# A fused cross-attention, Mamba and expert layer on one core: late matmul groups in the weighted values' PSUM bank, the joining of context blocks cut in four, three scalings in one step, first queries' transposes issued earlier

## The chip, the cores and the metric

One core of a Trainium2 chip. The kernel is one launch with no collectives. The metric is the device time of one execution in microseconds, as a median of repeated runs; beside it stands one profiled execution, from which all durations of single instructions are taken.

## The reference, cut to what matters

All data are fp32. Sixteen sequences of 128 rows and width 512 each attend to a context of 2048 rows; then each pair of sequences goes through a Mamba layer (a scan over time with 16 states for each of 1024 channels), an MLP, and a mixture of experts.

```python
x = x + xattn(layernorm(x), ctx)        # 16 heads of 32; q,k,v,o projections of 512x512
x = x + mamba_block(layernorm(x))       # in_proj, causal conv of 4, SiLU, dt/B/C, scan, out_proj,
                                        # rmsnorm, MLP 512-2048-512 with exact GELU, rmsnorm
x = x + experts(layernorm(x))           # shared matmul + expert matmul times a gate's weight
# attention, for sequence b:
q = layernorm(x[b]) @ wq.T + bq;  k = ctx[b] @ wk.T + bk;  v = ctx[b] @ wv.T + bv
out = softmax(q k^T / sqrt(32)) v  @ wo.T + bo
```

## The kernel before, in words

**Units.** The program is one long unrolled list. Its loop `for u in range(last)` writes one *unit* after the other; the first 256 (NU) are the attention's. Unit u works on sequence b = u // 16, on the context block of 512 rows sb = u // 4 % 4, and on the group of four heads hg = u % 4. A *row* below is the 16 units of one sequence; row 12 is units 192 to 207. Every engine takes its instructions strictly in the order in which they were written, under `tc.manual_schedule()`, so this loop is the schedule.

**What a unit issues, in order.** `scores` (L302): four matmuls q k^T into the four PSUM banks `banks[0..3]`. `weighted` of the unit before (L346): the probabilities times v, summed over a whole sequence's head group into the bank `avp`; after the fourth head group `avp` is copied to SBUF (`avs`, L360), which happens in units with u % 4 == 0. The `head` list. `maxima` (L310, VectorE): the negated row maximum of each of the four banks. `x_products` (L240): two products for the next context block's keys or values, into the banks `pa` and `pc` (a Strassen-Winograd scheme: seven products of quarter size for each of k and v, spread over units; its sums of context quarters t1 to t4 are GpSimd's, L232, in units with u % 4 == 1). `exps` (L320, ScalarE). Then the Mamba part of an earlier pair of sequences, which runs 22 units behind: `inputs` (L639, GpSimd), `decays` (L660, ScalarE), `scan` (L674 and L677, VectorE; L690, GpSimd). `x_sums` (VectorE, reads `pc`). `turn` (L333): the probabilities are transposed, four transposes for each of i = 0 to 3, each i into one of the four banks, and copied out as `pT` (L338, ScalarE; i = 2 on VectorE, L336, in units with u % 16 > 2). The lists `middle`, `late`, `behind`, `after`, `inner`. Last `y_products` (one or two more products) and `y_sums`, and `silu_second` (L565, VectorE).

**The lists.** `put(list, u, f)` hangs a piece of work on a unit. A `late` piece is a group of matmuls with its own PSUM result: in an attention unit it gets `banks[3]`, a second one `banks[0]`, and so on; only turns 0 to 2 go before it, and turn 3 is issued after it, into the bank behind the last one used. The late pieces are `turned` (L389, the normalised x transposed, copied out by VectorE as xnT, L391), `queries` (L399), `scaled` (L455, a factor for each head transposed, which VectorE multiplies onto `avs`, L460 and L462, and GpSimd adds up into aT, L463), `attended` (the output projection, L468), `z_turned` (L515), `x_part` and `z_part` (L522), `x_proj` (L576), `projected` (L703). `behind` (dt_first, L606) uses `pc`.

**The end of a sequence.** With e = 16 b + 16 the four blocks' maxima and sums are joined: `joined` gathers the maxima with four copies (L422), takes their minimum (L427) and the differences (L428); `shares` is an exponential; `joined_second` (L436 to L438) sums; `joined_third` (L443) divides. `spread_out` (L449, GpSimd) widens the factors into the tile `fx`, which has two buffers and also holds xnT.

**The start of a sequence.** With s = 16 b: load x at s - 8, `moments_of` (L66) at s - 7, `root_of` and `normal` (L83, L89 to L91, L376, and GpSimd's x + bo, L380) at s - 6, `turned` at s - 5, `queries` at s - 4. Sequence 0 has these in the stretch before the loop, where `turned(0, banks[3])` comes after the sums of the weights' quarters (`weight_sums`, L216 to L219) of k and of v.

**After the loop's attention part** the program goes on with the MLP, the experts and the last scans; there PSUM banks come from a free list.

Of the kernel before, what the change touches and what calls it, by code (L numbers as in the profile page):

```python
# [34 lines left out]
def perceiver_layer(ctx: ExitStack, tc: tile.TileContext, a: dict, out: bass.AP):  # L35
# [73 lines left out]
    with ExitStack() as es:  # L109
# [254 lines left out]
        def moments_of(b):  # L364
            moments(keep, mv[:, b, :], xts[b])
            xts[b, "r"] = root_first(keep, mv[:, b, 1:2], 1e-5)

        def root_of(b):
            root_second(*xts[b, "r"])

        def normal(b):

            x = xts[b]
            root_third(rstd[:, b : b + 1], *xts.pop((b, "r")))
            xn = keep.tile([P, D], FP, tag="aT", name="xn", bufs=1)
            nc.vector.tensor_scalar(  # L376
                xn, x, mv[:, b, 0:1], rstd[:, b : b + 1], ALU.subtract, ALU.mult
            )
            if b:
                nc.gpsimd.tensor_tensor(x, x, bo, ALU.add)  # L380
            xts[b, "n"] = xn
            nm = [keep.tile([P, SB, 4], FP, tag=f"nm{j}", name=f"nm{b}_{j}") for j in range(4)]
            sm = keep.tile([P, SB, H], FP, tag="sm", name=f"sm{b}")
            stats[b] = nm, sm

        def turned(b, ps):
            xn = xts.pop((b, "n"))
            for kc in range(KC):
                nc.tensor.transpose(heads(ps)[:, kc, :], xn[:, kc * P : (kc + 1) * P], ident)  # L389
            xnT = keep.tile([P, KC, P], FP, tag="fx", name="xnT")  # L390
            nc.vector.tensor_copy(xnT, heads(ps))  # L391
            xts[b, "t"] = xnT

# [23 lines left out]
        def joined(b):  # L417

            parts, sm = stats[b]
            nm = keep.tile([P, SB, H], FP, tag="nm", name=f"nm{b}")  # L420
            for j in range(4):
                nc.vector.tensor_copy(  # L422
                    nm.rearrange("p s (k j) -> p s k j", j=4)[:, :, :, j], parts[j]
                )
            lo = keep.tile([P, 1, H], FP, tag="lo", name="lo")
            flat = lo.rearrange("p a h -> p (a h)")
            nc.vector.tensor_reduce(flat, nm.rearrange("p s h -> p h s"), AX.X, ALU.min)  # L427
            nc.vector.tensor_tensor(nm, lo.to_broadcast([P, SB, H]), nm, ALU.subtract)  # L428
            stats[b] = nm, sm, lo, flat

        def shares(b):
            nc.scalar.activation(stats[b][0], stats[b][0], AF.Exp)
# [12 lines left out]
        fxs = {}  # L445

        def spread_out(b, sb):
            fx = keep.tile([P, H, HD], FP, tag="fx", name="fx")
            nc.gpsimd.tensor_copy(fx, stats[b][:, sb, :].unsqueeze(2).to_broadcast([P, H, HD]))  # L449
            fxs[b, sb] = fx.rearrange("p h d -> p (h d)")  # L450

# [199 lines left out]
        def anew(h):  # L651

            nc.vector.memset(h.rearrange("p n (b t) -> p (n b) t", b=GB)[:, :, 0:1], 0.0)  # L653
# [423 lines left out]
        def put(where, u, f):  # L1077
            where.setdefault(u, []).append(f)

        for b in range(B):  # L1080
            s = 16 * b
            if b:
                put(loads, s - 8, lambda b=b: load_x(b))
                put(loads, s - 5, lambda b=b: load_w(0, b))
                put(inner, s - 7, lambda b=b: moments_of(b))
                put(middle, s - 6, lambda b=b: root_of(b))
                put(inner, s - 6, lambda b=b: normal(b))
                put(late, s - 5, lambda ps, b=b: turned(b, ps))
                put(late, s - 4, lambda ps, b=b: queries(b, ps))
            e = s + 16  # L1090
            put(loads, e + 5, lambda b=b: load_w(3, b))
            put(inner, e - 1, lambda b=b: joined(b))
            put(middle, e, lambda b=b: shares(b))
            put(head, e + 1, lambda b=b: joined_second(b))
            put(head, e + 2, lambda b=b: joined_third(b))
            for sb in range(SB):
                put(inner, e + 2 + sb // 2, lambda b=b, sb=sb: spread_out(b, sb))
                put(late, e + 3 + sb // 2, lambda ps, b=b, sb=sb: scaled(b, sb, ps))
            put(late, e + 6, lambda ps, b=b: attended(b, ps))
            put(middle, e + 7, lambda b=b: root_of(b))  # L1100
            put(inner, e + 7, lambda b=b: normed(b))
            put(late, e + 8, lambda ps, b=b: z_turned(b, ps))
        for g in range(NG):
# [15 lines left out]
            for i in range(GB):  # L1119
# [2 lines left out]
                put(loads, s + 31 + 2 * i, lambda b=g * GB + i: reload_x(b))  # L1122
                put(late, s + 33 + 2 * i, lambda ps, g=g, i=i: projected(g, i, ps))

        put(inner, NU - 3, lambda: anew(pc))
        put(loads, NU - 20, load_normw)
        put(loads, NU - 5, lambda: load_z(0))
# [29 lines left out]
        normal(0)  # L1157
        first_sums("k", 0)
        first_products("v", 0)
        ctx_sums(0, ("t1", "t2", "t3", "t4"))  # L1160
        weight_sums("k")
        first_sums("v", 0)
        weight_sums("v")
        turned(0, banks[3])
        queries(0, banks[2])
        nc.scalar.activation(aneg, aneg, AF.Exp)
        nc.vector.tensor_scalar_mul(aneg, aneg, -1.0)
# [2 lines left out]
            y_sums(of, 0, 0, sa, sc, tag)  # L1170
        load_w(3, -1)

        bvx = keep.tile([P, KC, P], FP, tag="fx", name="bvx")
        nc.vector.tensor_copy(bvx, bv.unsqueeze(2).to_broadcast([P, KC, P]))
        for of, sa, sc, tag in ways:
            first_products(of, 1)
# [13 lines left out]
        for u in range(last):  # L1190
            live = u < NU
            g, r = divmod(u - 32 - LAG, 32)
            scans = 0 <= g < NG

            made, phase = divmod(u + 3, 4)
            makes = 0 < made < B * SB
            of, phase = ("k", "v")[phase // 2], phase % 2
            load_bc(u + 2 - 32 - LAG, 0)
            if u % 4 == 1 and made + 1 < B * SB:
                load_ctx(made + 1, ("c00", "c10", "c11"))  # L1200
            if u % 4 == 2 and made + 1 < B * SB:
                load_ctx(made + 1, ("c01",))
            for f in loads.get(u, ()):
                f()
            if scans:
                decays(g, r, 0)
            if u > NU:
                while fed < feeds * (u - NU) // (last - 1 - NU):
                    feed(fed)
                    fed += 1  # L1210
            load_bc(u + 1 - 32 - LAG, DS)
            if u == NU + 1:
                load_rows()
            if live:
                scores(u)
            if 1 <= u <= NU:
                weighted(u - 1)
            if u == NU:
                att.close()
                give_back(flat(pa), banks[2], banks[1], flat(avp))  # L1220
                open_ffn()
            if u == NU + 8:
                load_wex()
            for f in head.get(u, ()):
                f()
            if live:
                maxima(u)
            if makes:
                x_products(of, made, phase, pa, pc)
            if live:  # L1230
                exps(u)
            if makes and u % 4 == 1:
                ctx_sums(made, ("t1", "t2"))
            if 0 <= u + 1 - 32 - LAG < 32 * NG:
                inputs(*divmod(u + 1 - 32 - LAG, 32))
            if makes and u % 4 == 1:
                ctx_sums(made, ("t3", "t4"))
            silu_third()
            if scans:
                scan(g, r, 0)  # L1240
            if makes:
                hold(of, made, pa, "u1")
            if scans:
                decays(g, r, 1)
            if makes:
                x_sums(of, made, phase, pa, pc)


            after_turns = late.get(u, ())
            if live:  # L1250
                for i in range(3 if after_turns else 4):
                    turn(u, i, i)
            if scans:
                scan(g, r, 1)
            for f in middle.get(u, ()):
                f()
            for i, f in enumerate(after_turns):
                ps = banks[(3 + i) % 4] if live else bank()
                f(ps)
                if not live:  # L1260
                    give_back(ps)
            if live and after_turns:
                turn(u, 3, (3 + len(after_turns)) % 4)
            for f in behind.get(u, ()):
                ps = flat(pc) if makes else banks[2] if live else bank()
                f(ps)
                if not live:
                    give_back(ps)
            for f in after.get(u, ()):
                f()  # L1270
            for f in inner.get(u, ()):
                f()
            if makes:
                y_products(of, made, phase, pa, pc)
                y_sums(of, made, phase, pa, pc)
            silu_second()
# [76 lines left out]
```

## Time and profile before

| | us |
|---|---|
| median of 3 runs (3813.38 to 3817.05) | 3814.19 |
| the profiled execution, its own time | 3814.88 |
| its span, first to last instruction | 3813.1 |
| before unit 0 | 50.6 |
| units 0 to 31 | 333.3 |
| units 32 to 254 | 2726.6 |
| from unit 255 to the end | 702.5 |

Busy shares of the span: VectorE (DVE) 71%, ScalarE (ACT) 64%, GpSimd (POOL) 55%; TensorE's own line is shown with the prediction. The mean granted TensorE clock is 0.993 of full speed. DMA is busy 43%.

How to read it: a row of the timeline is start in us, length in us, engine, line, operation, out<-in, number of instructions, and in brackets the engine's idle time before it with what ended it. PE is a matmul, PEld a weight load. Neighbouring matmuls overlap, and a matmul's end is modelled, so lengths of matmul groups are best taken as the step from one group's start to the next group's start. Such steps repeat to a hundredth of a microsecond from row to row.

### The profile page before, as it was taken

What the parts mean: (1) busy time and instruction counts of PE and PEld (TensorE: products, weight loads), DVE (VectorE), ACT (ScalarE), POOL (GpSimd) and SP (SyncE); (2) the same over time, 40 slices, a digit from 0 to 9 for tenths busy, and PEclk for the clock granted to TensorE, in tenths of its full rate; (3) what the DMA queues carried; (4) which work ended last, traced back from release to release, by engine and by line L of the source; (5) the groups of instructions that cost most, each with busy time, mean ns of one, the idle gap of its engine ahead of it and who ended that gap; (6) DMA issues with size and microseconds to landing.
All of it is one profiled execution on the core that took longest, in us unless ns stands there. A gap on an engine that the chain in (4) does not pass through costs nothing.

```text
span 3813.1 us, 70343 instructions
## 1 busy us (share of the span) xinstructions
PE 3745.4 (98%) x26120; PEld 2854.8 (75%) x26120; DVE 2711.9 (71%) x4852; ACT 2449.0 (64%) x5847; POOL 2105.6 (55%) x1968
## 2 busy tenths in 40 slices
PE   8999999999999999999999999999999989999999
PEld 6878787778777877787778777787778766656555
DVE  3444445887878787878787778877887777767843
ACT  3555556777767776777677767776777665545421
POOL 2111113676657666766676666666665667567730
PEclk9999999999999999999999999999999999999999
DMA  3111122444444435353534353435344457577752
GB/s 93 42 34 45 51 68 83 130 147 146 135 163 144 153 120 175 131 162 111 188 128 147 124 191 117 155 130 180 130 153 136 153 179 274 190 256 261 260 191 72
DMA packets 341223, 548.40 MB, mean 144 GB/s; under 512 B 24432, under 2 KB 225408, under 8 KB 340624
## 3 DMA queue, kind: packets, MB, share of 16 engines
q1 hardware_dynamic: 340464, 543.28, 43.2%
q8 instruction: 206, 3.38, 0.4%
q14 instruction: 137, 1.12, 0.1%
q0 software_dynamic: 416, 0.63, 0.1%
HBM read 527.29 MB, written 16.52 MB: 143 GB/s over the span
## 4 chain that ended last, share of the span: by engine, by line
PE 85%; DVE 9%; ACT 3%; issue 2%; DMA 1%; POOL 0%; DVEq 0%; SPq 0%; ACTq 0%
PE pa L240 21%; PE pc L240 16%; PE bank L333 10%; PE bank L302 7%; PE avp L346 6%; PE bank L522 5%; PE bank L869 4%; PE bank L703 3%; DVE hst L674 2%; PE bank L838 2%; DVE nm L310 2%; PE bank L964 2%; PE bank L399 2%; DVE w L677 2%; PE bank L468 1%
## 5 line engine op out<-in xcount | busy, mean ns | idle before, releaser
L310 DVE TENSOR_REDUCE nm<-bank 128x1 f32<-128x512 f32 x1024 | 635.0, 682 | 243.0 <-PE bank L302 242.2
L690 POOL TENSOR_TENSOR ysum<-ysum,w 128x512 f32<-128x512 f32 x384 | 500.8, 1304 | 483.2 <-DVE hst L653 303.0
L320 ACT ACTIVATE pr<-bank,nm 128x512 f32<-128x512 f32 x1024 | 690.8, 688 | 98.4 <-DVE nm L310 92.8
L639 POOL TENSOR_TENSOR w<-dx,bc 128x512 f32<-128x512 f32 x512 | 649.9, 1291 | 3.8
L338 ACT COPY pT<-bank 128x512 f32<-128x512 f32 x816 | 438.2, 585 | 221.2 <-PE bank L333 217.2
L674 DVE TENSOR_TENSOR_SCAN hst<-hst,w 128x512 f32<-128x512 f32 x456 | 557.4, 1222 | 12.4 <-ACT hst L660 8.5
L333 PE MATMUL bank<-ident,pr 128*128 128x128 f32 x4096 | 524.9, 274 | 15.9 <-ACT pr L320 13.9
L660 ACT ACTIVATE hst<-dt,alog 128x254 f32<-128x254 f32 x912 | 436.7, 479 | 146.8 <-DVE hst L653 128.0
L333 PEld LDWEIGHTS bank<-ident,pr 128*128 128x128 f32 x4096 | 471.5, 142 | 74.3 <-ACT pr L320 21.8
L346 PEld LDWEIGHTS avp<-pT,v 128*32 128x32 f32 x8192 | 208.0, 109 | 194.2 <-issue 194.2
L677 DVE TENSOR_TENSOR w<-hst,bc 128x512 f32<-128x512 f32 x456 | 315.3, 692 | 23.8 <-DMA bc<-bcd 8.3
L302 PE MATMUL bank<-kt,qT 32*128 32x512 f32 x2048 | 298.4, 643 | 5.7 <-DVE avs L462 5.7
L232 POOL TENSOR_TENSOR t<-c,c 128x512 f32<-128x512 f32 x128 | 164.6, 1286 | 241.9 <-PE pc L240 236.5
L346 PE MATMUL avp<-pT,v 128*32 128x128 f32 x8192 | 276.7, 276 | 0.0
L240 PE MATMUL pa<-t,ks 128*128 128x256 f32 x1024 | 248.6, 386 | 0.0
L240 PE MATMUL pa<-vs,t 128*128 128x256 f32 x1008 | 244.7, 386 | 0.0
L522 PE MATMUL bank<-zT,win 128*128 128x256 f32 x968 | 220.8, 381 | 4.6 <-ACT hs L852 4.6
L240 PEld LDWEIGHTS pa<-vs,t 128*128 128x128 f32 x1008 | 185.4, 190 | 34.7 <-issue 10.1
L320 ACT ACTIVATION_READ_ACCUMULATOR pr<-bank,nm 128x1 f32 x1024 | 209.7, 205 | 0.0
L240 PEld LDWEIGHTS pa<-t,ks 128*128 128x128 f32 x1024 | 184.4, 190 | 32.4 <-issue 10.7
L336 DVE COPY pT<-bank 128x512 f32<-128x512 f32 x208 | 143.9, 692 | 88.9 <-PE bank L333 87.5
L522 PEld LDWEIGHTS bank<-zT,win 128*128 128x128 f32 x968 | 180.6, 191 | 28.4 <-ACT hs L852 5.0
(302 smaller groups left out, 6852.9 us busy)
## 6 DMA issues: line engine op xcount, KB each, us to landing
bc<-bcd SPq DMA_DIRECT2D x512, 512.0 KB, 4.3
c<-in_ctxT_dram SPq DMA_DIRECT2D x256, 256.0 KB, 4.4
wf<-in_w_dram SPq DMA_DIRECT2D x128, 512.0 KB, 7.1
wqo<-in_wqkvo_dram SPq DMA_DIRECT2D x128, 256.0 KB, 4.8
win<-in_win_dram SPq DMA_DIRECT2D x128, 256.0 KB, 4.4
wout<-in_wout_dram SPq DMA_DIRECT2D x128, 256.0 KB, 4.2
x<-in_x_dram SPq DMA_DIRECT2D x16, 256.0 KB, 4.2
x1d<-x SPq DMA_DIRECT2D x16, 256.0 KB, 2.1
```

The lines of the kernel that those rows point to most:

```text
L240: nc.tensor.matmul(ps[:, r, :], l[:, kc, r * P : (r + 1) * P], m[:, kc, :], start=(i in (1, 2, 5) and r == 0 and kc == 0), stop=(r == 1 an ...
L302: nc.tensor.matmul(banks[j], qts[b][rows, hg, :], kts[u // 4, hg][rows, :], start=True, stop=True)
L310: nc.vector.tensor_reduce(stats[b][0][j][:, sb, hg : hg + 1], banks[j], AX.X, ALU.max, negate=True)
L320: nc.scalar.activation(pr[:, j, :], banks[j], AF.Exp, bias=nm[j][:, sb, hg : hg + 1], accum_out=sm[:, sb, h : h + 1],)
L333: nc.tensor.transpose(ps[:, j, :], prs[u][:, j, i * P : (i + 1) * P], ident)
L338: nc.scalar.copy(pT, ps)
L346: nc.tensor.matmul(avp[j * HD : (j + 1) * HD, hg, :], vts[u // 4, hg // 2, i // 2][:, i % 2, hg % 2 * P + j * HD : hg % 2 * P + (j + 1) * HD],
L522: nc.tensor.matmul(ps, w[:, kc, :], zTs[g][:, kc, :], start=(kc == 0), stop=(kc == KC - 1))
L639: nc.gpsimd.tensor_tensor(w, dx.unsqueeze(1).to_broadcast([P, NH // 2, GT]), bcs[g * 32 + r, 0][:, i * NH // 2 : (i + 1) * NH // 2, :], AL ...
L660: nc.scalar.activation(bt(h[:, k, :])[:, :, 1:], bt(dt)[:, :, 1:], AF.Exp, scale=aneg[:, ec, n : n + 1],)
L674: nc.vector.tensor_tensor_scan(flat, flat, w.rearrange("p n t -> p (n t)"), 0.0, ALU.mult, ALU.add)
L690: nc.gpsimd.tensor_tensor(s, s, w, ALU.add)
```

## The change

- A late group no longer always takes a bank of the four. In units with u % 4 == 0 the first late group gets `avp`, which has just been copied out; in odd units that make keys or values and have no `behind` piece, the last late group gets `pc`. Turn 3 is held back only if a late group still takes one of the four banks.
- `joined` is cut: the four copies move to the head of unit e, minimum and differences (`joined_first`) to the inner list of e, `shares` to e + 1, `joined_second` from the head of e + 1 to its inner list; `joined_third` stays at the head of e + 2.
- Of the four scalings the first is alone in unit e + 3, and the other three come in e + 4 (before: two and two); the spreading follows the same split. The tile `fx` gets a third buffer.
- In the loop `moments_of`, `root_of`, `normal` and `turned` come one unit earlier each; `turned` is put last in its unit's late list; `queries` stays.
- Before the loop, `turned(0)` comes ahead of the sums of the weights.

```diff
-            xnT = keep.tile([P, KC, P], FP, tag="fx", name="xnT")
+            xnT = keep.tile([P, KC, P], FP, tag="fx", name="xnT", bufs=3)
...
                     nm.rearrange("p s (k j) -> p s k j", j=4)[:, :, :, j], parts[j]
                 )
+            stats[b] = nm, sm
+
+        def joined_first(b):
+            nm, sm = stats[b]
             lo = keep.tile([P, 1, H], FP, tag="lo", name="lo")
...
-                put(inner, s - 7, lambda b=b: moments_of(b))
-                put(middle, s - 6, lambda b=b: root_of(b))
-                put(inner, s - 6, lambda b=b: normal(b))
-                put(late, s - 5, lambda ps, b=b: turned(b, ps))
+                put(inner, s - 8, lambda b=b: moments_of(b))
+                put(middle, s - 7, lambda b=b: root_of(b))
+                put(inner, s - 7, lambda b=b: normal(b))
                 put(late, s - 4, lambda ps, b=b: queries(b, ps))
...
-            put(inner, e - 1, lambda b=b: joined(b))
-            put(middle, e, lambda b=b: shares(b))
-            put(head, e + 1, lambda b=b: joined_second(b))
+            put(head, e, lambda b=b: joined(b))
+            put(inner, e, lambda b=b: joined_first(b))
+            put(middle, e + 1, lambda b=b: shares(b))
+            put(inner, e + 1, lambda b=b: joined_second(b))
             put(head, e + 2, lambda b=b: joined_third(b))
             for sb in range(SB):
-                put(inner, e + 2 + sb // 2, lambda b=b, sb=sb: spread_out(b, sb))
-                put(late, e + 3 + sb // 2, lambda ps, b=b, sb=sb: scaled(b, sb, ps))
+                put(inner, e + 2 + (sb > 0), lambda b=b, sb=sb: spread_out(b, sb))
+                put(late, e + 3 + (sb > 0), lambda ps, b=b, sb=sb: scaled(b, sb, ps))
...
+        for b in range(1, B):
+            put(late, 16 * b - 6, lambda ps, b=b: turned(b, ps))
...
         first_products("v", 0)
+        turned(0, banks[3])
         ctx_sums(0, ("t1", "t2", "t3", "t4"))
         weight_sums("k")
         first_sums("v", 0)
         weight_sums("v")
-        turned(0, banks[3])
         queries(0, banks[2])
...
             after_turns = late.get(u, ())
+            places = [banks[(3 + i) % 4] for i in range(len(after_turns))]
+            if live and after_turns:
+                if u % 4 == 0:
+                    places = [flat(avp), *places[:-1]]
+                elif u % 2 and makes and u not in behind:
+                    places[-1] = flat(pc)
+            taken = sum(any(p is b for b in banks) for p in places)
             if live:
-                for i in range(3 if after_turns else 4):
+                for i in range(3 if taken else 4):
                     turn(u, i, i)
...
-            if live and after_turns:
-                turn(u, 3, (3 + len(after_turns)) % 4)
+            if live and taken:
+                turn(u, 3, (3 + taken) % 4)
```

More of the change, by code (lines that the diff above doesn't have):

```diff
@@ L447, in spread_out @@
         def spread_out(b, sb):
-            fx = keep.tile([P, H, HD], FP, tag="fx", name="fx")
+            fx = keep.tile([P, H, HD], FP, tag="fx", name="fx", bufs=3)
             nc.gpsimd.tensor_copy(fx, stats[b][:, sb, :].unsqueeze(2).to_broadcast([P, H, HD]))
@@ L1171, in perceiver_layer @@
         load_w(3, -1)
-        bvx = keep.tile([P, KC, P], FP, tag="fx", name="bvx")
+        bvx = keep.tile([P, KC, P], FP, tag="fx", name="bvx", bufs=3)
         nc.vector.tensor_copy(bvx, bv.unsqueeze(2).to_broadcast([P, KC, P]))
@@ L1256, in perceiver_layer @@
                 f()
[L1257 to L1260, printed above, removed]
+            for f, ps in zip(after_turns, places):
+                if live:
+                    f(ps)
+                else:
+                    ps = bank()
+                    f(ps)
                     give_back(ps)
-            if live and after_turns:
-                turn(u, 3, (3 + len(after_turns)) % 4)
+            if live and taken:
+                turn(u, 3, (3 + taken) % 4)
             for f in behind.get(u, ()):
```

## The prediction, made before the changed kernel was run

> **What bounds the kernel now.** I read the page first, then TensorE's waits, then the timeline of the stretch before the loop, then the timeline unit by unit.
>
> ```profile
> span 3813.1 us, 70343 instructions
> ...
> PE 3745.4 (98%) x26120; PEld 2854.8 (75%) x26120; DVE 2711.9 (71%) x4852; ACT 2449.0 (64%) x5847; POOL 2105.6 (55%) x1968
> ...
> PE 85%; DVE 9%; ACT 3%; issue 2%; DMA 1%; POOL 0%; DVEq 0%; SPq 0%; ACTq 0%
> ```
>
> TensorE sets the time and the change leaves its 26120 matmuls alone, so only TensorE's stalls can move. Its waits:
>
> ```profile
> PE bank L333 <- ACT pr L320: 13.9, 23, 6.1
> PE bank L399 <- DVE xnT L391: 9.5, 1, 9.5
> ...
> PE bank L302 <- DVE avs L462: 5.7, 12, 0.5
> ```
>
> One wait of 9.5 us stands before the loop. For the loop I took the step from each matmul group's start to the next group's and subtracted the smallest step of the same group anywhere (scores 1.07, four turns 1.75, a late group of four transposes 0.44). What is left is stall, and it repeats every 32 units. In units 192 to 223: unit 192 1.00; 195 and 211 0.57 each; 196 and 212 0.16 each; 200 0.50; 208 0.17; 210 0.14; 216 0.10; 220 0.39; together 3.76 us. Six such pairs and a first row (48 to 63) with 1.96 make about 24 us, which with the 9.5 is all that the change can win.
>
> **Before the loop.**
>
> ```profile
> 14.29 1.63 DVE L216 TENSOR_TENSOR ks<-ks,ka 128x512 f32<-128x512 f32 x1 [3.04 <-DMA ka<-in_wqkvo_dram]
> ...
> 21.09 0.69 DVE L217 TENSOR_TENSOR vs<-vs,va 128x512 f32<-128x512 f32 x1
> ...
> 22.91 0.69 DVE L391 COPY xnT<-bank 128x512 f32<-128x512 f32 x1
> ...
> 23.65 6.35 PE L399 MATMUL bank<-xnT,wqo 128*128 128x128 f32 x32 [9.48 <-DVE xnT L391]
> ...
> 31.35 1.70 PEld L240 LDWEIGHTS bank<-vs,t 128*128 128x128 f32 x8
> ```
>
> xnT is queued on DVE behind nine sums. Moved ahead of them, it runs from 14.2 (its transposes end at 14.17) to 14.9. L216 then starts 0.6 later, but it was waiting for a GpSimd sum that ends at 15.38 (L216 ended 0.5 after that), so the chain of sums does not shift and `vs` is still ready at 21.8. The queries now wait for their weights, which land at 16.6, 17.5, 18.4 and 19.3. At the loop's pace (3.57 for 32 matmuls) the last quarter ends at about 20; the key product fits in until 21.8 and the value product starts at 21.9 in place of 31.35: 9.4 us won. What comes next is TensorE-bound up to unit 0.
>
> The doubt is the clock. Before, the queries took 6.2, not 3.57:
>
> ```profile
> 14.00:23.50 9.50, 0.17 (x2) 0.00 (x0) 9.14 (x10) 0.00 (x0) 4.63 (x4) 0.75 0.71 195
> 23.50:30.00 6.50, 6.35 (x33) 6.35 (x34) 0.09 (x1) 0.00 (x0) 0.00 (x0) 0.58 0.31 82
> ```
>
> The third column from the right is the granted clock. It was halved for about half of the first window, so from about 18.7, some 4.7 us into the idleness, and stayed low for 5 us of work. By that row slow queries end at 16.7 + 6.2 = 22.9, the value product starts at 24.7, and 6.7 us are won. [...] I take 9.4 and keep 6.7 as the lower bound.
>
> **The joining, rows that start at a multiple of 32.** All of it stood ahead of unit 192's maxima:
>
> ```profile
> 2335.72 1.27 POOL L690 TENSOR_TENSOR ysum<-ysum,w 128x512 f32<-128x512 f32 x1 [2.99 <-DVE hst L653]
> 2336.01 1.46 DVE L422 COPY nm<-nm 128x16 f32<-128x16 f32 x4
> ...
> 2338.61 2.47 DVE L310 TENSOR_REDUCE nm<-bank 128x1 f32<-128x512 f32 x4
> ...
> 2342.16 1.64 PE L333 MATMUL bank<-ident,pr 128*128 128x128 f32 x13 [0.34 <-ACT pr L320]
> ```
>
> Unit 192's scores start at 2335.51, so its maxima start 3.10 after them instead of the usual 1.16. They were 1.94 late and cost 1.00, so about 0.94 of lateness is free. With only the copies ahead they start at 2337.47, 0.80 late: the stall falls to 0.05. The rest (L427 0.26 and L428 0.9) goes to the end of unit 192, where DVE has a free microsecond in front of unit 193's maxima because the sums (1.2) leave that place; those move to the end of unit 193 and finish with L443 just before unit 194's maxima are due.
>
> **The joining, rows that start 16 later (208).** L565 follows at the end of unit 207 and now comes ahead of the copies. In these rows every such SBUF-only DVE instruction ends 0.04 to 0.29 after the GpSimd instruction that was running. L565 then goes in when the first L639 ends, the copies must wait out the second, and the maxima start about 0.4 later than before: stall 0.17 to 0.57. Two units on, 0.14 becomes about 0.05.
>
> **Scalings.** In unit 195 one transposed factor stays, in `banks[3]`, and its product is on DVE right after L677. That is how `turned` stands in unit 219 before, which cost the scores of unit 220 0.39; so 0.57 becomes 0.39, not 0. In unit 196 the three go to `avp`, `banks[3]` and `banks[0]`; every bank's reader is done in time and the 0.16 goes. But GpSimd now adds three times in one go:
>
> ```profile
> 2389.95 2.68 POOL L463 TENSOR_TENSOR aT<-aT,avs 128x512 f32<-128x512 f32 x2
> ...
> 2396.24 1.28 POOL L232 TENSOR_TENSOR t<-c,t 128x512 f32<-128x512 f32 x1
> ...
> 2398.03 1.89 PE L240 MATMUL pa<-t,ks 128*128 128x256 f32 x8
> ```
>
> Behind the adds are queued three updates of dt, then t1 and t2, which TensorE needs in unit 197. t2 ends at 2397.52, 0.51 before it is needed. A third add costs 1.34, less 0.27 by which unit 196 is longer: 1.07 late, 0.51 of it free, so a new stall of about 0.6 in units 197 and 213. Twelve rows have it; in unit 53 t2 is early by 2.6.
>
> **Late groups in `avp` and `pc`.** Units 200 and 216 waited for turn 0's copy before turn 3; with z_turned in `avp` all four turns come first and 0.50 and 0.10 go. Products put into `pc` or `avp` elsewhere (`z_part`, `x_part`, `projected`, `queries`) had no stall to lose; their readers are done 3 us or more before the next writer.
>
> **First norm and transposes a unit earlier.** `turned` leaves unit 219, so unit 220's 0.39 goes. In unit 218 (and 90, 122, 154, 186) turn 3 now follows in `banks[0]`, whose copy is late there:
>
> ```profile
> 2275.45 1.91 PE L333 MATMUL bank<-ident,pr 128*128 128x128 f32 x16
> 2276.51 0.49 ACT L668 ACTIVATE xa<-xa,dskip 128x256 f32<-128x256 f32 x1
> 2276.91 1.54 ACT L338 COPY pT<-bank 128x512 f32<-128x512 f32 x3
> ```
>
> Turn 0's copy ends 2.05 after the turns' start; turn 3 would go at 1.75: 0.3 of stall. The normalisation, moved behind `projected` in unit 217, makes the maxima of 218 about 0.5 late, and turn 0's copy with them: about 0.75 in all, 0.3 and 1.3 as ends. The load of x and its DMA queue keep their places; x lands some 5 us before its moments. In the other rows `turned` is last of three and its bank's neighbours are free: nothing.
>
> **The sum.** A pair of rows after: 0.05 + 0.39 + 0.60 (197) + 0.57 + 0.05 + 0.39 + 0.60 (213) + 0.75 (218) = 3.40 against 3.76. Six pairs win 2.2, the last row (no 218 or 220) 0.4 more, row 48 about 0.6: 3.2. With 9.4 it is 12.6. The profiled execution took 3814.88, 0.7 above the median of 3814.19; from the median, 3801.6, rounded to 3802.
>
> **Rivals.**
> *Everything clears* (0.12): the stalls of 197 and 213 (7.2) and of 208 and 218 (about 7) do not appear. For it: the margins are tenths of a microsecond. Against it: t2's lateness follows from one queue's order. 3802 - 15 = 3787.
> *The gain is mostly given back* (0.30): a slow clock in the queries (6.7), or 218 and 208 at their upper ends (0.6 and 0.4 more in five and six rows, 5.4). Then 4 to 7 are won: 3809.
> [...]
> The likeliest case (0.50) has a range of its own of 3796 to 3807. That the changed order is not what runs is excluded: the built program has the new places.
>
> **Chances and range.** 0.2%, 7.6 us, is about what a measurement of this kernel can tell from no change. Faster: nearly all of the likeliest case and all of the first rival, 0.61; slower 0.08; the rest, 0.31, is within. The range 3794 to 3814 takes the likeliest case, the second rival's lower gains, and leaves out most of the first and the third.
>
> **What would show it.** Queries start at 16.7 and the granted clock tells which of 9.4 and 6.7; unit 0 starts near 41.2; no wait of turns for `pr` in unit 192; L302 still waits 0.39 in unit 196; t2 ends after TensorE asks for it in 197 and 213; turn 3 of unit 218 waits for a `pT` copy. It is wrong if the waits of L240 for GpSimd are missing, or if unit 193, 194 or 209 stalls.

## The result, and the profile after

The changed kernel takes 3806.51 us (median of 15 runs, 3802.58 to 3810.12), the kernel before 3815.03 beside it (15 runs, 3812.00 to 3817.61): a ratio of 0.998, 95% interval 0.9972 to 0.9988, so 8.5 us won where 12.6 were forecast. In the profiled executions the span fell from 3813.1 to 3807.2, by 5.9.

The page of the changed kernel, span, busy time and the shares of the chain:

```profile
span 3807.2 us, 70317 instructions
...
PE 3747.0 (98%) x26120; PEld 2858.7 (75%) x26120; DVE 2690.4 (71%) x4852; ACT 2443.9 (64%) x5847; POOL 2107.1 (55%) x1968
...
PE 90%; DVE 5%; ACT 3%; issue 1%; POOL 1%; DMA 1%; SPq 0%; DVEq 0%; POOLq 0%; ACTq 0%
```

TensorE still sets the end, and DVE's share of the chain went from 9 to 5%. TensorE's waits (us in total, times, longest us):

```profile
PE pa L240 <- POOL t L232: 6.1, 12, 0.5
...
PE bank L333 <- ACT pT L338: 3.3, 6, 1.3
PE bank L399 <- DMA wqo<-in_wqkvo_dram: 3.0, 1, 3.0
...
PE pa L873 <- DVE avs L466: 1.1, 1, 1.1
```

The wait of 9.5 us for xnT is a wait of 3.0 for weights, the waits for DVE's scalings are gone from the list, and twelve waits for GpSimd's t2 are new. The list holds only gaps ahead of a matmul: the 0.39 us that the scores of units 196 and 212 still lose lie inside their group and do not show in it. Turns wait for copies of `pT` six times with 3.3 us in all; before it was seven times with 2.0. (The lines of the changed kernel that are named here have numbers 4 higher than before from the old line 427 on.)

I cut each execution in three: up to the start of unit 0, from there to the start of unit 255, and the rest of the span.

| | before | after | difference | forecast |
|---|---|---|---|---|
| start of unit 0 | 50.63 | 43.67 | -6.96 | -9.4 |
| unit 0 to unit 255 | 3059.87 | 3057.97 | -1.90 | -3.2 |
| unit 255 to the end | 702.6 | 705.6 | +3.0 | 0 |

**The start.** The timeline of the changed kernel (start, duration, engine, line, and in brackets idle time and who ended it):

```profile
14.69 0.69 DVE L391 COPY xnT<-bank 128x512 f32<-128x512 f32 x1 [3.46 <-PE bank L389]
...
17.60 5.44 PE L399 MATMUL bank<-xnT,wqo 128*128 128x128 f32 x32 [2.95 <-DMA wqo<-in_wqkvo_dram]
...
21.91 0.69 DVE L217 TENSOR_TENSOR vs<-vs,va 128x512 f32<-128x512 f32 x1
...
24.39 0.62 PEld L240 LDWEIGHTS bank<-vs,t 128*128 128x128 f32 x3
```

xnT is copied 8 us earlier and `vs` is ready at 22.6, but the queries take 5.3 us (17.60 to 22.87, where the key product starts) and not 3.6, and hold back the key product and with it the value product: 24.39 instead of the 21.9 of the forecast. In the table by stretches (TensorE, its weight loads, DVE, ACT, GpSimd, then the granted clock, the share of DMA and GB/s):

```profile
18.00:19.00 1.00, 1.00 (x9) 1.00 (x8) 1.00 (x2) 0.00 (x0) 1.00 (x1) 0.73 1.17 321
19.00:20.00 1.00, 1.00 (x7) 1.00 (x6) 1.00 (x2) 0.00 (x0) 0.53 (x1) 0.50 0.93 327
20.00:21.00 1.00, 1.00 (x7) 1.00 (x6) 1.00 (x3) 0.00 (x0) 0.00 (x0) 0.50 0.71 203
21.00:22.00 1.00, 1.00 (x7) 1.00 (x7) 0.97 (x3) 0.00 (x0) 0.00 (x0) 0.56 0.44 141
22.00:24.00 2.00, 2.00 (x16) 1.87 (x15) 1.81 (x3) 0.93 (x4) 0.00 (x0) 1.00 0.70 216
```

The clock was halved from about 18.5 to 21.9, although TensorE had only been idle from 14.65 to 17.60 and was at work again when it fell.

**The loop.** In unit 192 the copies alone stand ahead of the maxima, which start 1.86 after the scores (3.10 before), and all sixteen transposes follow without a break, where before 13 of them stood behind a wait of 0.34:

```profile
2328.45 1.45 DVE L422 COPY nm<-nm 128x16 f32<-128x16 f32 x4
...
2329.80 2.47 DVE L310 TENSOR_REDUCE nm<-bank 128x1 f32<-128x512 f32 x4
...
2333.58 1.91 PE L333 MATMUL bank<-ident,pr 128*128 128x128 f32 x16
```

In unit 197 the third addition shows. The row of the additions was 2.68 for two and is 4.11 for three; t2, the later of the two L232, ends at 2389.78, 8.01 after the unit's scores started instead of 6.88, and TensorE waits:

```profile
2380.79 4.11 POOL L467 TENSOR_TENSOR aT<-aT,avs 128x512 f32<-128x512 f32 x3
...
2388.50 1.28 POOL L232 TENSOR_TENSOR t<-c,t 128x512 f32<-128x512 f32 x1
...
2389.83 1.99 PE L240 MATMUL pa<-t,ks 128*128 128x256 f32 x8 [0.52 <-POOL t L232]
```

Unit 58, for which the forecast had no entry of its own, stalls 2.55 where it was 0.91:

```profile
687.59 0.76 DVE L376 TENSOR_SCALAR xn<-x,mv,rstd 128x512 f32<-128x512 f32 x1
...
688.28 1.49 DVE L569 SCALAR_TENSOR_TENSOR sg<-zs,sg 128x256 f32<-128x256 f32 x1
...
689.69 2.47 DVE L310 TENSOR_REDUCE nm<-bank 128x1 f32<-128x512 f32 x4
...
694.28 0.60 PE L389 MATMUL bank<-ident,xn 128*128 128x128 f32 x4
...
696.19 0.66 PE L333 MATMUL bank<-ident,pr 128*128 128x128 f32 x4 [1.31 <-ACT pT L338]
```

The same unit before (its scores start at 693.78):

```profile
695.34 1.34 DVE L565 SCALAR_TENSOR_TENSOR sg<-zs,sg 128x256 f32<-128x256 f32 x1
...
696.60 2.47 DVE L310 TENSOR_REDUCE nm<-bank 128x1 f32<-128x512 f32 x4
```

The normalisation L376 now stands ahead of L569 (L565 before) there, and the maxima start 3.38 after the scores (686.31), 0.56 later than the 2.82 of before. L569, which takes 0.41 where nothing is in its way, ended only after GpSimd's two sums in both kernels, so this was lost before, too. Most of the new stall is turn 3's: from the start of the transposes L389 to its own 1.91 us pass, where 0.44 is the least. It now stands behind them and goes into the bank of turn 0, whose copy ScalarE makes late; before, no late group stood in this unit and no turn had to wait for a copy.

### The profile page after: what moved, and what is told of

It is laid out like the page before. It is cut to its first block, busy times and chain, and to the rows that moved or that the text cites. A ratio compares the mean times of both kernels' runs of the same rounds, so it can differ in the third digit from the quotient of the medians.

```text
span 3807.2 us, 70317 instructions
## 1 busy us (share of the span) xinstructions
PE 3747.0 (98%) x26120; PEld 2858.7 (75%) x26120; DVE 2690.4 (71%) x4852; ACT 2443.9 (64%) x5847; POOL 2107.1 (55%) x1968
## 3 DMA queue, kind: packets, MB, share of 16 engines
q8 instruction: 206, 3.38, 0.4%
## 4 chain that ended last, share of the span: by engine, by line
PE 90%; DVE 5%; ACT 3%; issue 1%; POOL 1%; DMA 1%; SPq 0%; DVEq 0%; POOLq 0%; ACTq 0%
PE pa L240 24%; PE pc L240 17%; PE bank L333 11%; PE bank L302 7%; PE avp L346 6%; PE bank L526 4%; PE bank L873 3%; PE bank L968 2%; PE bank L842 2%; PE bank L472 2%; PE avp L399 1%; PE bank L707 1%; PE pc L707 1%; PE pa L873 1%; PE pc L526 1%
## 5 line engine op out<-in xcount | busy, mean ns | idle before, releaser
L232 POOL TENSOR_TENSOR t<-c,c 128x512 f32<-128x512 f32 x128 | 164.4, 1285 | 259.4 <-PE pc L240 253.2
L232 POOL TENSOR_TENSOR t<-c,t 128x512 f32<-128x512 f32 x128 | 163.4, 1276 | 36.5 <-issue 19.6
L526 PE MATMUL bank<-zT,win 128*128 128x256 f32 x792 | 182.7, 381 | 0.0
```

Of the source, the lines that this page charges most:

```text
L526: nc.tensor.matmul(ps, w[:, kc, :], zTs[g][:, kc, :], start=(kc == 0), stop=(kc == KC - 1))
```

## The experiments

The theory: about 7 us come from the start, 2 from the loop, and part of it is lost behind the loop. Its rival: the loop's edits bring the gain. "Loop" below is the time from the start of unit 0 to that of unit 255 in the profiled execution, which repeats far better than the whole. Each ratio is to runs of the kernel before on the same chip; where a time is set against the changed kernel's, that is its 3806.51, for which the kernel before had 3815.03.

**Only the start.** In the kernel before:

```
         first_products("v", 0)
+        turned(0, banks[3])
         ctx_sums(0, ("t1", "t2", "t3", "t4"))
...
         weight_sums("v")
-        turned(0, banks[3])
```

> The kernel before with one edit: the transposes of the first normalised block stand ahead of the weight sums. Theory (about 7 of the 8.5 us come from before the loop): 7.0 us faster than before, 3808; unit 0 starts near 43.7, and the loop from unit 0 to unit 255 takes what it took before, within 0.5. Rival (the gain comes from the joining and the places in the loop, and the start is only moved about): within 2 us of before, since what is won at the start is lost on the way, for instance because the loads of the loop come out of step.

Measured: 3806.74 us beside 3815.35, ratio 0.9977 (0.9968 to 0.9986); loop 3059.77, within 0.1 of before. The one moved line brings 8.6 us, as much as the whole change: the theory holds, with 1.6 more than it said. Unit 0 starts at 41.65, 2 us earlier than in the changed kernel, because here the clock stayed whole, with the weights awaited for 2.34 us and the queries done in 3.65:

```profile
17.50:19.00 1.50, 1.50 (x16) 1.50 (x15) 1.50 (x2) 0.00 (x0) 1.50 (x1) 1.00 1.22 301
19.00:20.00 1.00, 1.00 (x12) 1.00 (x11) 1.00 (x2) 0.00 (x0) 0.13 (x1) 1.00 1.01 352
```

**All but the start.** The changed kernel with that line put back behind the sums.

> The changed kernel with the transposes of the first block back behind the weight sums: all edits but that of the start. Theory (7 to 9 us come from the start, about 2 from the loop, and the scalings of the last block, three in one unit, cost 1.4 behind the loop): within 2 us of before, 3813 to 3815; unit 0 starts near 50.6, the stretch from unit 0 to unit 255 takes 1.9 less than before. Rival (the edits of the loop bring a good part of the gain, and the start's gain is partly lost behind it): 4 us or more faster than before.

Measured: 3815.98 beside 3815.50, ratio 1.0003 (0.9995 to 1.0011); unit 0 starts at 51.21 and the loop takes 3058.10, 1.8 less than before. All the loop's edits together change nothing that can be measured. The rival falls.

**Two and two scalings.** In the changed kernel:

```
-                put(inner, e + 2 + (sb > 0), lambda b=b, sb=sb: spread_out(b, sb))
-                put(late, e + 3 + (sb > 0), lambda ps, b=b, sb=sb: scaled(b, sb, ps))
+                put(inner, e + 2 + sb // 2, lambda b=b, sb=sb: spread_out(b, sb))
+                put(late, e + 3 + sb // 2, lambda ps, b=b, sb=sb: scaled(b, sb, ps))
```

> The changed kernel with the four scalings two and two again, as before. Theory (the third addition on GpSimd makes t2 late in units 197 and 213, 0.78 in twelve places): the waits of L240 for L232 go, 9.4 us; units 195 and 211 get their 0.57 back, which is 6.8, and units 196 and 212 fall from 0.39 to 0.16 or stay, so 2.6 to 5.4 us faster than the changed kernel, 3801 to 3804. Rival (the stall of 197 has another cause, such as the spreading of three factors in the unit before or the later joining): 0.5 us or more of stall stays in units 197 and 213 and the kernel is 4 us or more slower than the changed one.

Measured: 3800.47 beside 3815.35, ratio 0.9958 (0.9944 to 0.9971), 6.0 below the changed kernel; loop 3051.08, 6.9 less. In each of twelve rows 0.78 goes in unit 197 (or 213), 0.39 in 196 (212), and 0.57 comes back in 195 (211): 12 x 0.60 = 7.2. I had expected the 0.39 to stay in part. So the scaling split of one and three is a loss by itself.

**Only the spreading two and two** (the first of those two lines alone, one run).

> The changed kernel with only the spreading of the factors two and two again; the scalings and additions stay one and three. Theory (the third addition is what makes t2 late): units 197 and 213 keep their 0.78. Rival (it is the third spreading of factors in the unit before): most of the 0.78 goes.

Measured: 3808.22 in one run; loop 3058.38, 0.4 from the changed kernel's, and units 197 and 213 keep 0.78. So it is not the spreading; what is left is the row of three additions, 4.11 us long instead of 2.68.

**The first norm a unit later.** In the changed kernel:

```
-                put(inner, s - 8, lambda b=b: moments_of(b))
-                put(middle, s - 7, lambda b=b: root_of(b))
-                put(inner, s - 7, lambda b=b: normal(b))
+                put(inner, s - 7, lambda b=b: moments_of(b))
+                put(middle, s - 6, lambda b=b: root_of(b))
+                put(inner, s - 6, lambda b=b: normal(b))
...
-            put(late, 16 * b - 6, lambda ps, b=b: turned(b, ps))
+            put(late, 16 * b - 5, lambda ps, b=b: turned(b, ps))
```

> The changed kernel with the moments, the root, the normalisation and the transposes of a block's first norm one unit later, as before. Theory (units 90, 122, 154, 186 and 218 stall 0.62 because the transposes stand there, and unit 58 1.6 more than before): these 4.7 us go, 0.39 comes back in six units that follow the transposes, 2.3; so 2 to 2.5 us faster than the changed kernel, 3804. Rival (the stall of unit 58 is a late turn of GpSimd's that the joining or the scalings bring, and has nothing to do with the norm): unit 58 keeps its 2.5, and the kernel is within 1 us of the changed one.

Measured: 3804.85 beside 3815.35, ratio 0.9969 (0.9958 to 0.9981). The loop takes 3054.68, 3.3 less than the changed kernel's. Two parts of that hang on the clock and not on the edit: 1.1 is won in units 0 and 1 (see below), and 0.8 is lost in units 253 and 254, where the clock fell 17.6 us ahead of unit 255 and in the changed kernel only 7.8. The remaining 3.0 is what was tested: units 48 to 63 win 2.1, for unit 58 falls to 0.05; five rows win 0.2 each, since 0.62 goes in unit 218 and its like while 0.39 comes back two units on. The stall of unit 58 belongs to the moved norm and its transposes. What of the 0.62 is the late maxima and what the wait for a bank was not separated.

**Transposes in the wait.** In the changed kernel, with work added that the result doesn't use:

```
         turned(0, banks[3])
+        for _ in range(32):
+            nc.tensor.transpose(heads(banks[2])[:, 0, :], ident, ident)
```

> The changed kernel with 32 more transposes of the identity, whose results nothing reads, on TensorE between the transposes of the first block and the queries, so that TensorE hardly idles while it waits for the weights. Theory (the clock was halved from 18.5 to 21.9 and made the queries 5.2 instead of 3.6): the granted clock stays at 1.00, the queries end 0.9 after their last quarter of weights lands, the value product starts 1.0 to 1.7 earlier and the kernel is as much faster, 3805. Rival (the queries are slow because their weights land one by one, 0.9 apart): the clock makes no difference, and the queries end when they did; 0 to 0.3 us.

Measured: 3806.72 beside 3815.35, ratio 0.9977 (0.9966 to 0.9987): no gain over the changed kernel. The granted clock is 1.00 from the transposes to the end of the queries, the queries take 3.57, and unit 0 starts at 42.49, 1.2 earlier. That the transposes kept the clock is not shown by this: without them the wait would have been 2.4 us, and waits of 2.01 to 2.67 left the clock whole in four executions without them. That the rival is wrong was shown by the kernel with only the start moved: 3.65 us for the queries at a whole clock, while their weights landed one by one. The transposes also cost something: they end at 18.1, and weights that land at 17.1 must wait for them: against executions in which the clock stays up anyway (unit 0 at 41.5 to 41.7) they lose 0.9. This kernel's stretch behind unit 255, whose code is that of the changed kernel, took 701.1 and not 705.6.

**The joining in one place.** The changed kernel with the copies and what follows them again at the end of unit `e - 1`, and `shares` and `joined_second` in unit `e` and ahead of the maxima of `e + 1`:

```
-            put(head, e, lambda b=b: joined(b))
-            put(inner, e, lambda b=b: joined_first(b))
-            put(middle, e + 1, lambda b=b: shares(b))
-            put(inner, e + 1, lambda b=b: joined_second(b))
+            put(inner, e - 1, lambda b=b: joined(b))
+            put(middle, e, lambda b=b: shares(b))
+            put(head, e + 1, lambda b=b: joined_second(b))
```

> The changed kernel with the joining of the blocks in one place again. Theory (the split joining takes away 1.00 of stall in units 64, 96, 128, 160, 192 and 224, some in unit 48, and adds 0.14 in units 80, 112, 144, 176, 208 and 240): 5 to 6 us slower than the changed kernel, 3812. Rival (the joining's gain shows again a few units later, as lateness that another wait takes up): 2 us or less.

Measured: 3813.22 beside 3815.25, ratio 0.9994 (0.9986 to 1.0002); loop 3063.09, 5.1 more than the changed kernel's. Unit 192 stalls 1.0 again and 208 only 0.17. The split joining is worth its 5 us; the rest of the loop's edits spend it.

**The scores' banks alone.** The changed kernel without

```
-            if live and after_turns:
-                if u % 4 == 0:
-                    places = [flat(avp), *places[:-1]]
-                elif u % 2 and makes and u not in behind:
-                    places[-1] = flat(pc)
```

> The changed kernel with the late groups in the scores' banks alone, so that neither the weighted values' bank nor that of the products takes any. Theory (the place in the weighted values' bank takes away 0.50 in units 200, 72, 104, 136, 168, 232 and 0.10 in 216 and its like): 3 to 4 us, and in unit 196 three scalings in banks 3, 0 and 1 add 0.2 to 1.0 in twelve places; 6 to 14 us slower than the changed kernel, 3812 to 3820. Rival (the places make no difference because the readers of the scores' banks are done in time anyway, and DVE's late products are what the scores wait for): within 2 us.

Measured: 3810.59 beside 3815.25, ratio 0.9987 (0.9980 to 0.9993); loop 3060.95, 3.5 more than the changed kernel's when what hangs on the clock (1.1 won in units 0 and 1, 0.6 lost in units 253 and 254) is put aside. The 0.50 in unit 200 and the 0.10 in 216 are back as expected. Three scalings in banks 3, 0 and 1 cost 0.20 in unit 196, but unit 197 then stalls 0.59 instead of 0.78: t2 was late anyway, so that lateness is paid once. My 6 to 14 counted it twice.

**One, two, one.** In the changed kernel `(sb > 0)` becomes `(sb + 1) // 2` in both lines.

> The changed kernel with one scaling in units 195 and 211, two a unit later and one two units later, the factors spread a unit ahead each. Theory (three additions in one unit cost 0.78 in twelve places; a second transposed factor in units 195 and 211 costs 0.57, one costs 0.39 a unit later): the 0.78 go and the 0.39 stay, so 8 to 9.4 us less than the changed kernel in the loop, and about 2 less than with two and two; with the scalings of the last block spread too, 3797. Rival (any addition in the unit before t1 and t2 makes them late): units 197 and 213 keep 0.3 or more, or unit 198 stalls because the fourth addition now delays the inputs of the scan; 3800 or more.

Measured: 3842.57 beside 3815.25, ratio 1.0071 (1.0058 to 1.0083), 36 us slower than the changed kernel. Units 197 and 213 stall no more, as the theory said, but 198 and 214 stall 3.0 to 4.7. The fourth addition's inputs are ready early in unit 198, and yet it stands in GpSimd's queue behind everything that ends a row of the scan; the output projection waits for it:

```profile
2418.31 0.73 POOL L699 TENSOR_TENSOR zs<-ysum,zs 128x256 f32<-128x256 f32 x1
2418.99 1.27 POOL L467 TENSOR_TENSOR aT<-aT,avs 128x512 f32<-128x512 f32 x1
...
2420.31 2.08 PE L472 MATMUL bank<-wqo,aT 128*128 128x512 f32 x2 [2.72 <-POOL aT L467]
```

My rival had the place right and the mechanism wrong: the scan's inputs were not what was late.

**The fourth addition on DVE.** As above, with the first norm a unit later, the 32 transposes, and

```
-                nc.gpsimd.tensor_tensor(avs[b], avs[b], t, ALU.add)
+                eng = nc.vector if sb == 3 else nc.gpsimd
+                eng.tensor_tensor(avs[b], avs[b], t, ALU.add)
```

> One, two and one scalings as in the run that lost 36 us, but the fourth addition on DVE in place of GpSimd; the first norm one unit later, and 32 idle transposes ahead of the queries as in the run with them. Theory (the 2.7 of each output projection were a wait for the fourth addition, queued on GpSimd behind the end of a scan): units 198 and 214 lose nothing, units 197 and 213 lose nothing, 0.39 stays in 196 and 212; 3794 to 3797. Rival (DVE has no room for an addition ahead of the maxima of unit 198): 0.5 or more of stall in units 198 and 214, 3800 or more.

Measured: 3792.15 beside 3815.50, ratio 0.9939 (0.9925 to 0.9953), and no stall in 197, 198, 213 or 214; loop 3045.45, 12.5 less than the changed kernel's. With that one instruction on another queue the 3.0 to 4.7 of all twelve rows are gone.

**Two and two, with the first norm a unit later and the 32 transposes.**

> Two and two scalings, the first norm one unit later, and 32 idle transposes ahead of the queries: three of the tried edits together. Theory (their gains are in different units and add up): 6 from the scalings, 2 from the norm, and up to 1.5 from the clock in executions in which it fell, so 3797 to 3799. Rival (they share a gain): no faster than two and two alone, 3800.5.

Measured: 3794.69 beside 3815.50, ratio 0.9946 (0.9933 to 0.9958). The gains lie in different units and add up: the loop takes 3047.80, 10.2 less than the changed kernel's, and 6.9 and 3.0 make 9.9. That the median lies 2 us below the forecast has no explanation here.

**Twelve transposes.** The kernel with the fourth addition on DVE, with `range(12)`.

> The kernel with the fourth addition on DVE, with 12 idle transposes ahead of the queries in place of 32. [...] Rival (only an unbroken row of transposes up to the queries keeps the clock): 0.50 for some 3.4 us between 17.5 and 22, unit 0 near 43.5, no gain.

Measured: 3790.62 beside 3813.97, ratio 0.9940 (0.9927 to 0.9954). The queries start at 16.87 as their weights land, the clock is 1.00, and unit 0 starts at 41.31 instead of 43.30. Part of these 2 us is chance, since the first weights landed at 16.73 in this execution and at 17.64 in the other; the 32 transposes held the queries back by a further 1.2. That the twelve transposes kept the clock is not shown by it: without them the wait would have been 2.7 us, and after one of 2.67 (the kernel with the joining in one place) the clock stayed at 1.00 without any. The medians, 1.5 apart, were not taken beside each other and have nearly the same ratio, so a gain over 32 transposes is not shown. The kernel beats both kernels, 23 us below the one before.

## Why the prediction was right or wrong

The 3806.5 lies in the range of 3794 to 3814 and just inside the likeliest case's own (3796 to 3807), between its 3802 and the 3809 of the rival in which the gain is mostly given back. The first of the two reasons that this rival named came true, but its sum was wrong: a slow clock alone leaves 6.7 + 3.2 = 9.9 and not 4 to 7. The rest was lost in the loop and behind it.

**The start: the step that failed is the clock.** The order of the work came as forecast; the first weights landed at 17.5 and not 16.6, and `vs` was ready at 22.6 and not 21.8. I then had two sums, 9.4 with a whole clock and 6.7 with a slow one, and chose 9.4 on the assumption that an idle stretch of 2.6 us leaves the clock up. No run shows that it always does; the runs showed a start of unit 0 between 6.6 and 9.1 us earlier. Both sums are near what came: where the clock stayed up (the kernel with only the start moved, and those with one-two-one, with the joining in one place and with the scores' banks alone) unit 0 starts at 41.5 to 41.7, 9.0 to 9.1 us earlier than before; where it fell (the changed kernel, two and two, the norm a unit later, the even spreading) at 43.1 to 44.1, 6.6 to 7.5 earlier. The 6.7 is right in part by luck: it let the queries start at 16.7 and take 6.2, and in the changed kernel they started at 17.60 and took 5.3, to the same end at 22.9. The choice between them could not be made in advance: the clock stayed up in the four kernels whose weights were awaited for 2.01 to 2.67 us and fell in the four with 2.95 to 3.22, and the same instructions before the loop gave either. The forecast should have had the middle, about 8.

In the clock records of the kernel before and of the changed one, every halved stretch but the last, which the end of the trace cuts off, lasts 3.41, 6.83, 10.24 or 17.07 us; at the start it was 10.24 (18.70 to 28.94) before and 3.41 (18.46 to 21.87) after. Equal waits had different ends (last section).

**The loop: right in nearly every unit.** Per pair of rows, stalls in us:

| unit | forecast | measured |
|---|---|---|
| 192 (and 194) | 0.05 | 0.00 + 0.05 |
| scores of 196, of 212 | 0.39 each | 0.39 each |
| 197, 213 | 0.60 each | 0.78 each |
| 208 | 0.57 | 0.31 |
| 210 | 0.05 | 0.14 |
| 218 | 0.75 | 0.62 |
| 200, 216, 220 | 0 | 0 |
| sum | 3.40 | 3.46 |

The sum is right in part because its errors cancel. The most costly mis-sized term is the third addition: I gave it 1.34 less 0.27, and t2 ended 1.13 later against its unit, not 1.07. Less the 0.51 that was free, this is 0.62; the product starts 0.05 after t2 ends, and it takes 0.10 more from its start to the next group's than one that did not wait (1.92 instead of 1.82), which makes 0.77. In unit 208 the maxima start only 0.14 later than before against the scores (2.67 instead of 2.53), not 0.4. Nearly all of the 1.3 us by which the loop fell short lies in units 48 to 63: forecast 0.6 won, measured 0.7 lost, through unit 58. I had put the price of transposes ahead of turn 3 in 218 and its like, at 0.75; unit 58 is such a unit, too, and had none. There turn 0's copy came later than in 218, and the step of the transposes grew by 1.48, not by the 0.57 that it grew by there. (About 0.4 of the 1.9 that the loop won is not the edits': it lies in unit 254, where the clock fell at different times in the two executions: it was halved in the unit's first 1.3 us and from 8.2 on before, and from 6.2 on after.)

**Behind the loop: a step I left out.** I costed the three scalings in twelve rows and not for the last block, whose scalings run in unit 260, where the scores are done. There TensorE waits 1.1 for DVE (the L873 row above). Aligned with the kernel before, each of the seven profiled executions with three scalings in one unit loses 1.38 us between 3158 and 3180 of before's time, and each of the six others 0.02 or less. The remaining 1.6 of the 3.0 is not the change's: the kernels of this study took 700.0 to 708.0 behind unit 255, and the one that differs only in 32 transposes far ahead took 4.5 less than the changed kernel.

**The sum.** 7 to 9 at the start, 1.9 in the loop and -1.4 behind it make 7.5 to 9.5; 8.5 was measured, and the start alone brings 8.6. The 0.08 of a slower kernel rested on turns that GpSimd's additions would lose to DVE; no run shows such a loss: in unit 197 t2 came 1.13 later, for one addition more of 1.34. GpSimd did make a kernel slower, the one-two-one kernel by 36 us, but there its queue's order decided, not the time of the work in it.

## What to carry to other kernels

Where TensorE waits a few microseconds for a transfer, ask what the clock does next, and price both answers. A handful of idle transposes in the wait is worth a trial, if they end before the transfer does; in all four executions with them the clock stayed up, but the waits there would have been 2.2 to 2.9 us without them, so that they are what kept it is not shown. Work given to an engine with time to spare is cheap only if what is queued ahead of it there is done when its reader needs it: the same addition made TensorE wait 2.7 us a time on GpSimd and not at all on DVE. And when several edits are measured as one, run each of them out: here the gains of two edits (about 5 and 3.5 us when each is taken out alone) were spent by two others (about 7 and 3, and 1.4 behind the loop; they overlap in some units, so the figures do not add up exactly), and one moved line outside the loop was left as the whole result.

## What the hardware showed that I had not expected

The length of a wait alone did not tell whether the clock fell. The one-two-one kernel repeats the same wait of 2.7 us twelve times, 32.7 us in all, and the clock did not do the same after each. Two of the twelve, the output projections of two rows, the first without a fall (granted clock 1.00 from 1023.5 to 1037.5) and the second with one:

```profile
1031.43 3.70 PE L472 MATMUL bank<-wqo,aT 128*128 128x512 f32 x8 [2.69 <-POOL aT L467]
```

```profile
1221.76 5.40 PE L472 MATMUL bank<-wqo,aT 128*128 128x512 f32 x8 [2.73 <-POOL aT L467]
```

and the granted clock in the stretch of the second (the column before the last two):

```profile
1219.00:1222.00 3.00, 0.27 (x2) 0.24 (x2) 2.58 (x4) 1.02 (x3) 2.92 (x4) 0.98 0.00 1
1222.00:1225.40 3.40, 3.40 (x5) 1.32 (x5) 0.00 (x0) 0.00 (x0) 3.37 (x3) 0.52 0.00 0
1225.40:1228.00 2.60, 2.60 (x12) 1.54 (x11) 0.78 (x2) 0.37 (x1) 2.50 (x2) 1.00 0.00 0
```

One stretch of 3.4 us at 0.52 of the clock, and 1.7 us more for the same eight matmuls (5.40 instead of 3.70). What decides between the two is not shown by these runs.

The clock is also part of what sets the profiled executions apart: units 0 and 1 take 1.1 us more where the clock falls in unit 0 (in the changed kernel it was halved from 49.18 to 52.59), and behind the loop a wait of 2.6 us for a weight, which was 1.9 in the kernel before, put the kernel of all but the start 2.4 us back, where the clock fell (0.84 and 0.81 in the stretches 3405 to 3410 and 3410 to 3415), and the kernel of two and two scalings 0.7, no more than the waits differ.
